# Second attention of a two-layer transformer: one product for the maxima of four heads, a start by groups, and gathers that wait for their tiles

## The chip, the core and the metric

The kernel runs on one core of one Trainium2 chip. The metric is the time of one execution on the device in microseconds (us); a median of several runs is given. The engines are TensorE (PE; its weight loads PEld), VectorE (DVE), ScalarE (ACT), GpSimd (POOL) and SyncE (SP, which here only issues DMAs). Each engine works through its own queue in order, and they wait for each other by semaphores.

## What is computed

x is 64 batches of 128 tokens of 128 channels, in float32. Two layers follow each other:

```
x = x + cross_attention(layernorm(x), keys/values from fside and ctx)      # 16 heads of 8, 248 keys
x = x + experts(layernorm(x))      # 8 experts, the two best of each token, SwiGLU
x = x + cross_attention(layernorm(x), keys/values from ctx)                # 16 heads of 8, 120 keys
x = x + experts(layernorm(x))      # 8 experts, the two best, GELU, rank 64
```

The attention of each is softmax(q k / sqrt(8)) v, with biases on q, k, v and the output.

## The kernel before

**Batches and groups.** `attention(layer, w, norm, first, aside)` (L228) is a generator that serves both layers; `first` tells the first from the second. A group is GB = 4 batches, and there are 16 groups (NG). One iteration `it` of its loop advances a software pipeline: maxima of batch `it`, shift of batch `it-1`, scores and exponentials of `it-2`, values of `it-3`, output steps of `it-3` to `it-5`. The order of instructions on PE, ACT, DVE and POOL is that of the code (a manual schedule); the two sets of work beside the attention (`Aside0`, `Aside1`) are called at fixed places of the iteration: routing, experts, norms, additions of gathered rows.

**Heads in row groups.** The 128 channels are four groups of 32 rows of the PE array (`ra`), with four heads each (`s`, NS = 4). A head's 8 channels lie among the 32 rows. The queries are kept four times, in `q4`, each masked by `hmask` to one head's channels (`prep_q`, L293). The keys are kept twice, in `K2` (`keys_of`, L207, on ACT), with `v = s // 2`; `K2` also has a row of ones through which the maxima are subtracted.

**Maxima and scores.** `max_bank` (L373) multiplies, for one row group, each of four masked queries with the keys of the batch: in the second attention 4 products of 120 columns into one PSUM bank, from which DVE takes four maxima per query (L385). `score_bank` (L401) does keys times shifted masked queries, two products of 256 columns; ACT takes the exponential (L409). `round_` pairs two row groups that do maxima with two that do scores; `rounds(0, 1)` of the second attention fills all eight PSUM banks. PSUM tiles come in turn from `mtile()`, eight banks.

**Shift.** `shift` (L430, L433) turns the maxima with two PE transposes, and DVE adds them into `q4`. The scores of that batch, in the next iteration's rounds, read it.

**Order in the second attention's iteration.** values and `out1` (L446, L455), `rounds(0, 1)`, one piece of the experts (L1385 to L1418), `prep(it, 0)`, `out3`, `out2` (L475, L462, L466, L468), `out4` (L482), a router call, `prep(it, 1)`, `shift`, `out5` (L487), norms and gathers. `prep` makes the next group ready: with j = it mod 4, keys at j = 1 (L202, L207), values and transposed inputs at j = 2 (L214, L221, L176, L177), queries at j = 3 (L289, L293).

**Start.** The second attention starts with `prep_batch(0)`, and makes its first four batches ready one by one in iterations 0 to 2 (L313 to L318); group 1 comes in iterations 1 to 3.

**Between the attentions.** `tile_stage` runs the first layer's experts over 71 tiles of 256 rows: SP fetches rows from `xs` (L1051), PE multiplies (L1085, L1098), and the results go to `ys` in DRAM (L1105). POOL had scattered the rows into `xs` by indirect DMAs (L783). Within it, `first_results` gathers the results of the first 8 batches from `ys` (L1127, POOL), adds them (L1139) and makes the norms of two groups. The gathers of the others (L1328) and their additions (L1340) run beside the second attention. The dependencies of scatters, fetches and first gathers are given by hand: a declaration that none is there in a group of instructions, and a helper `behind` that adds single ones. `lists_`, `rp`, `yb` are pools of buffers in SBUF.

Of the kernel before, what the change touches and what calls it, by code (L numbers as in the profile page):

```python
# [44 lines left out]
def transformer_kernel(ctx, tc, a, out):  # L45
# [34 lines left out]
    def attention_weights(p, names=("wq", "wk", "wv", "wo", "bq", "bk", "bv", "bo")):  # L80
        columns = {"bq": NS, "bk": NV}
        return {
            n: load_row(p + n, D) if n in ("bv", "bo")
            else load_const(p + n, [D, columns.get(n, D)], a[p + n])
            for n in names
        }
# [145 lines left out]
    def attention(layer, w, norm, first, aside):  # L232
# [5 lines left out]
        with ExitStack() as es:  # L238
# [9 lines left out]
            nm = NM  # L248

            src, q4s, xnTs, ps_, pavs, pts, ots, normed = {}, {}, {}, {}, {}, {}, {}, {}  # L250

# [23 lines left out]
            def mtile():  # L275
                return banks.tile([128, 512], F32, name="bank", tag="bank")

            def prep_x(g):
                xnT = work.tile([D, GB * S], F32, name="xnT", tag="xnT", bufs=1)
                norm.turned(normed.pop(g), mtile(), xnT)  # L280
                xnTs[g] = xnT
                q4s[g] = work.tile([128, GB, NS, S], F32, name="q4", tag="q4", bufs=3)

            pqs = {}

            def prep_q(g, v):
                if v == 0:
                    pqs[g] = mtile()
                    nc.tensor.matmul(pqs[g], lhsT=w["wq"], rhs=xnTs[g], start=True, stop=True)  # L289
                pq = pqs[g]  # L290
                for i in range(2):
                    s = 2 * v + i
                    nc.scalar.activation(  # L293
                        q4s[g][:, :, s, :], pq.rearrange("p (b q) -> p b q", b=GB),
                        AF.Identity, bias=w["bq"][:, s : s + 1], scale=hmask[:, s : s + 1],
                    )

            def prep_k(g):
                keys_of(w, src[g], g, n0, mtile())

            def prep_v(g):
# [21 lines left out]
            def prep(it, half):  # L323

                g, j = it // GB + 1, it % GB
                if not first:
                    if g == 1:
                        if (j, half) == (2, 1):
                            prep_v(1)
                        elif (j, half) == (1, 0):  # L330
                            prep_k(1)
                    elif g < NG:
                        pieces = (
                            (), (lambda: prep_k(g),),
                            (lambda: prep_v(g), lambda: prep_x(g)),
                            (lambda: prep_q(g, 0), lambda: prep_q(g, 1)),
                        )[j]
                        if half < len(pieces):
                            pieces[half]()
                    return  # L340
# [25 lines left out]
            def max_bank(b, ra, v):  # L366
# [5 lines left out]
                def mm(u, s):  # L372
# [8 lines left out]
                    for p in range(2)  # L381
                ]

                def reduce():
# [116 lines left out]
            if first:  # L501
                loads(0)
                yield
                context_k(0)
                yield
                context_v(0)
                loads(1)
                yield
                prep_k(0)
                prep_batch(0)  # L510
                yield
            else:
                prep_batch(0)
                loads(1)
            oTs, pos_ = {}, {}

            for it in range(B + 5):
# [13 lines left out]
                if first and it % GB == 2:  # L531
                    norm_of(it // GB + 2)
                if 2 <= it <= B + 1:
                    ps_[it - 2] = work.tile([128, nc_, 4, 512], F32, name="p", tag="p")
# [23 lines left out]
                else:  # L558
# [4 lines left out]
                    aside.piece(mtile)  # L563
                    if it < GB - 1:
                        prep_batch(it + 1)
                    prep(it, 0)
# [8 lines left out]
                    if it > GB and it % GB == 1:  # L575
                        norm_of(it // GB + 1)
                    if it == GB - 1:
                        normed[1] = READY[1]
                        prep_x(1)
                        prep_q(1, 0)  # L580
                        prep_q(1, 1)
                    aside.fetch_for(it)
# [184 lines left out]

    AFTER = mybir.DependencyInfo(mybir.DependencyClass.Sync, mybir.DependencyReason.DATA)
    DEEP = 4
    scatters, spare = [], []  # L770

    def behind(ins, earlier):
        for e in earlier:
            tc.add_manual_dep(ins.ins, e.ins.name, AFTER, reason="rows of one array")

    def scatter(probe, j, k, xn):
# [9 lines left out]
        if scatters:  # L786
            tc.declare_no_dep(s.ins, group="scatters", reason="rows of their own")
        behind(s, [scatters[-DEEP] if len(scatters) >= DEEP else spare[0]])
        tc.add_to_no_dep_group("scatters", s.ins)
# [50 lines left out]

    lists_ = ctx.enter_context(tc.tile_pool(name="lists", bufs=1))
    back = place.tile([S, B, 2], I32, name="back", tag="back")
# [179 lines left out]
    def tile_stage(work, mtile):  # L1022
# [14 lines left out]
        def fetch(t):  # L1037
# [9 lines left out]
            share = s[:, n + 3 * TT : n + 3 * TT + 2].rearrange("p (h d) -> p h d", h=2)  # L1047
            first_ = scatters[2 * GA * GB - DEEP : 2 * GA * GB]
            assert len(first_) == DEEP
            for dst, src in ((x, xs[bass.ds(r, TT), :D]), (share, xs[bass.ds(r, TT), bass.ds(e + D, 1)])):  # L1050
                f = nc.sync.dma_start(dst, src.rearrange("(h p) d -> p h d", p=S))  # L1051
                if t < NA:

                    tc.declare_no_dep(f.ins, group="scatters", reason="rows of the first groups")
                    behind(f, first_)
                    tc.add_to_no_dep_group("scatters", f.ins)
# [56 lines left out]
        def first_results(t):  # L1113
# [6 lines left out]
            if step == 0:  # L1120
# [4 lines left out]
                for b in range(2):  # L1125
                    for k in range(2):
# [3 lines left out]
                        )  # L1130
                        tc.declare_no_dep(g.ins, group="writes", reason="other tiles")
                        behind(g, needed)
                        groups.add("reads")
# [124 lines left out]

    rp = ctx.enter_context(tc.tile_pool(name="route", bufs=1))

# [26 lines left out]
    for g in range(4, NG):  # L1287
        load_x(g)
    l1 = attention_weights("a1_")
    wr1 = load_const("wgT", [D, E], a["wgT"])  # L1290
# [10 lines left out]
    with tc.manual_schedule(engines=ORDERED | {ET.SP}):  # L1301
        for _ in steps:
            pass


    class Aside1:


        def __init__(self, pool):
            self.pool, self.got, self.b, self.xn = pool, {}, 2 * GB, READY[0]  # L1310
            self.xnTs, self.gates, self.ready = {}, [], []
# [10 lines left out]
        def fetch(self, n):  # L1322
            for b in range(self.b, min(self.b + n, B)):
                if b % 2 == 0:
                    self.got[b // 2] = self.pool.tile([S, 2, 2, D], F32, name="yb", tag="yb", bufs=5)
                y = self.got[b // 2]
# [17 lines left out]

        def normed(self, j):

            return self.xn

        def made(self, b):
# [11 lines left out]
        def xnT_of(self, g):  # L1361
            self.xnTs[g] = self.pool.tile([D, GB * S], F32, name="xnT", tag="xnT", bufs=4)
            return self.xnTs[g]
# [81 lines left out]
def _laid_out(inp):  # L1445
# [29 lines left out]
    for p, l, names, tr in (  # L1475
# [6 lines left out]
        o[p + "wq"], o[p + "wk"] = moved(wq), moved(wk)  # L1482
        o[p + "bq"] = np.where(hm > 0, moved(bq).T, np.float32(0.0))
        o[p + "bk"] = np.where(km > 0, moved(bk).T, sm)
        o[p + "wv"], o[p + "bv"] = wv, bv
# [46 lines left out]
```

## Time and profile before

| What | us |
|---|---|
| Median of 3 runs (lowest, highest) | 1597.97 (1597.46, 1599.05) |
| The profiled execution | 1601.67 |
| Its span, first to last instruction | 1599.9 |
| Mean granted PE clock over the span | 0.959 |
| Second attention's share of the span, from its first transpose at 988.2 | 611.7 |
| L373, second attention: passes of 120 columns x2048 | 168.2 busy |
| L385, second attention: reductions x256 | 152.2 busy |
| L401, second attention: passes of 256 columns x2048 | 304.7 busy |

A row of the profile names line, engine, operation, what is written from what, shapes and count, then the busy time, the mean duration and the idle time of the engine ahead of it with what ended it. The time line gives start, duration and the merged count; in brackets stands the idle time before it. The slices show 40 equal parts of the span, and PEclk is the granted clock of PE in tenths. Busy times of matmuls overlap, since four row groups can work at once.

### The profile page before, as it was taken

How to read it: one execution, taken by the hardware profiler on the slowest of the kernel's cores; microseconds unless marked ns; L12 is line 12 of the kernel's file. 1: busy time of each engine (PE TensorE's matmuls, PEld its weight loads, DVE VectorE, ACT ScalarE, POOL GpSimd, SP SyncE). 2: the span in 40 equal slices, each digit the busy share in tenths (PEclk: the TensorE clock that was granted, in tenths of full speed). 3: DMA queues.
4: the chain of work that ended last, by engine and by line, in shares of the span. 5: the costliest groups of instructions: out<-in, count | busy, mean ns of one | idle time of the engine just before them, and what ended most of it. 6: DMA issues, size and time to landing. Idle time of an engine off the chain costs nothing.

```text
span 1599.9 us, 45004 instructions
## 1 busy us (share of the span) xinstructions
PE 1484.9 (93%) x18162; PEld 1182.0 (74%) x18162; DVE 1084.0 (68%) x2960; ACT 843.9 (53%) x1739; POOL 641.1 (40%) x1195
## 2 busy tenths in 40 slices
PE   7989999999999999888999998988999999999987
PEld 5767777777777777777888887767777777777765
DVE  6757888888888986454744443677666666667753
ACT  4646666666666655432333333666555555555643
POOL 4122255555565535443020302366554544443210
PEclk9999999999999999999999999799999989999999
DMA  8842122222222221466776664110111100000000
GB/s 218 228 115 59 48 57 56 62 60 60 60 60 59 53 71 44 133 190 186 202 212 193 201 186 127 30 32 21 37 31 29 31 29 28 27 27 15 15 8 27
DMA packets 143586, 133.22 MB, mean 83 GB/s; under 512 B 48402, under 2 KB 125970, under 8 KB 141458
## 3 DMA queue, kind: packets, MB, share of 16 engines
q1 hardware_dynamic: 135186, 113.02, 25.7%
q0 software_dynamic: 8192, 17.32, 3.5%
q8 instruction: 144, 2.36, 0.6%
q14 instruction: 64, 0.52, 0.1%
HBM read 97.31 MB, written 32.97 MB: 81 GB/s over the span
## 4 chain that ended last, share of the span: by engine, by line
PE 73%; DVE 10%; DMA 4%; issue 3%; SPq 3%; POOL 3%; ACT 3%; another core or an unknown queue 0%; POOLq 0%; ACTq 0%; DVEq 0%
PE bank L401 12%; PE bank L373 12%; PE bank L446 9%; PE bank L1085 9%; PE bank L1413 4%; PE bank L1392 4%; PE bank L1098 3%; DVE nm L385 3%; PE bank L289 2%; SPq L1247 2%; PE bank L1402 2%; PE bank L482 2%; DMA q<-xs 2%; PE bank L214 2%; PE bank L652 2%
## 5 line engine op out<-in xcount | busy, mean ns | idle before, releaser
L385 DVE TENSOR_REDUCE nm<-bank 128x2 f32<-128x496 f32 (+1 forms) x768 | 465.9, 664 | 141.3 <-PE bank L401 69.5
L401 PE MATMUL bank<-q,k 32*120 32x256 f32 (+1 forms) x3072 | 478.0, 408 | 16.4 <-DVE nm L385 5.0
L409 ACT ACTIVATE p<-bank 120x512 f32<-120x512 f32 (+1 forms) x768 | 403.3, 605 | 140.5 <-PE bank L401 106.0
L373 PE MATMUL bank<-k,q 32*128 32x248 f32 (+1 forms) x4096 | 462.4, 345 | 13.3 <-DMA k<-in_ctx_k 7.1
L373 PEld LDWEIGHTS bank<-k,q 32*128 32x128 f32 x4096 | 351.8, 191 | 81.6 <-issue 36.3
L401 PEld LDWEIGHTS bank<-q,k 32*120 32x120 f32 (+1 forms) x3072 | 302.0, 182 | 45.9 <-DVE nm L385 16.0
L446 PE MATMUL bank<-p,v 128*32 128x128 f32 (+1 forms) x4096 | 179.3, 279 | 4.6 <-DVE nm L385 3.9
L1090 DVE TENSOR_TENSOR p<-p,bank 128x256 f32<-128x256 f32 x213 | 87.8, 420 | 125.3 <-ACT p L1089 106.9
L155 POOL TENSOR_SCALAR rstd<-mv 128x4 f32<-128x4 f32 x32 | 6.3, 198 | 384.9 <-DVE mv L113 296.4
L783 POOL DMA_INDIRECT xs<-xn,at x128 | 129.4, 1011 | 28.5 <-issue 24.9
L455 ACT COPY ov<-bank 128x256 f32<-128x256 f32 x128 | 47.9, 375 | 170.5 <-PE bank L446 141.3
L1089 ACT ACTIVATE p<-bank 128x256 f32<-128x256 f32 x213 | 80.8, 385 | 102.4 <-PE bank L1085 92.4
L446 PEld LDWEIGHTS bank<-p,v 128*32 128x32 f32 (+1 forms) x4096 | 111.4, 111 | 29.6 <-issue 13.0
L1085 PE MATMUL bank<-q 128*128 128x256 f32 x516 | 122.4, 388 | 4.4 <-ACT oT L477 4.4
L433 DVE SCALAR_TENSOR_TENSOR q<-bank,c_smask,q 128x256 f32<-128x256 f32 x256 | 111.4, 477 | 12.7 <-PE bank L430 11.9
L1328 POOL DMA_INDIRECT yb<-ys,back x112 | 108.8, 971 | 27.7 <-issue 20.1
L167 POOL TENSOR_SCALAR xn<-x,mv,rstd 128x128 f32<-128x128 f32 x252 | 110.2, 447 | 7.5 <-issue 1.4
L293 ACT ACTIVATE q<-bank,c_a_bq,c_hmask 128x512 f32<-128x512 f32 x120 | 87.4, 787 | 45.3 <-PE bank L289 45.2
L1085 PEld LDWEIGHTS bank<-q 128*128 128x128 f32 x516 | 97.5, 196 | 17.0 <-ACT oT L477 4.8
L446 PE MATMUL bank<-p,vc 120*32 120x128 f32 x2048 | 104.2, 272 | 0.6 <-issue 0.5
L138 POOL TENSOR_TENSOR mv<-st 128x4 f32<-128x4 f32 x31 | 6.4, 206 | 205.4 <-DVE st L109 205.4
L1085 PE MATMUL bank<-vc 128*128 128x256 f32 x336 | 77.2, 379 | 0.0
(220 smaller groups left out, 2364.5 us busy)
## 6 DMA issues: line engine op xcount, KB each, us to landing
q<-in_w SPq DMA_DIRECT2D x43, 576.0 KB
vc<-in_w SPq DMA_DIRECT2D x28, 576.0 KB
vc<-in_ctx_v SPq DMA_DIRECT2D x16, 960.0 KB
ys<-zero SPq DMA_DIRECT2D x71, 128.0 KB
k<-in_ctx_k SPq DMA_DIRECT2D x32, 240.0 KB
q<-xs SPq DMA_DIRECT2D x43, 128.0 KB
ys<-q SPq DMA_DIRECT2D x43, 128.0 KB
x<-in_x SPq DMA_DIRECT2D x16, 256.0 KB
```

Of the source, the lines that this page charges most:

```text
L167: nc.gpsimd.tensor_scalar(xn[:, j, :D], xg[g][:, j, :], self.mv[:, b, 0:1], self.rstd[:, b : b + 1], ALU.add, ALU.mult,)
L293: nc.scalar.activation(q4s[g][:, :, s, :], pq.rearrange("p (b q) -> p b q", b=GB), AF.Identity, bias=w["bq"][:, s : s + 1], scale=hmask[:, ...
L373: nc.tensor.matmul(pa[:, u, :], lhsT=q4s[g][r, j, s, :], rhs=k2[g % 2][r, s // 2, j, :], start=True, stop=True,)
L385: nc.vector.tensor_reduce(nm[b % 2].rearrange("q i (a s) -> q a i s", s=16)[:, 2 * ra + v : 2 * ra + v + len(slots) // 2, :, 0], pa.rearra ...
L401: nc.tensor.matmul(pb[:n, v * 256 : (v + 1) * 256], lhsT=k2[g % 2][r, v, j, k0 : k0 + n], rhs=q4s[g][r, j, 2 * v : 2 * v + 2, :].rearrange ...
L409: nc.scalar.activation(ps_[b][:n, c, ra, :], pb[:n], AF.Exp, scale=SCALE)
L433: nc.vector.scalar_tensor_tensor(q, pm, smask[:, v : v + 1], q, ALU.mult, ALU.add)
L446: nc.tensor.matmul(pav[32 * ra : 32 * ra + 32, v * S : (v + 1) * S], lhsT=vs[g % 2][c][:, j, 4 * v + ra, i, :], rhs=p[:n, c, ra, (2 * v + ...
L783: s = nc.gpsimd.indirect_dma_start(xs, bass.IndirectOffsetOnAxis(at[:, j, k : k + 1], 0), xn, None)
L1085: nc.tensor.matmul(ph[:, u, :], lhsT=w[:, c, u * 128 : (u + 1) * 128], rhs=xT, start=True, stop=True)
L1090: nc.vector.tensor_tensor(hT[:, c, :], sa, ph[:, 1, :], ALU.mult)
L1328: nc.gpsimd.indirect_dma_start(y[:, k, b % 2, :], None, ys, bass.IndirectOffsetOnAxis(back[:, b, k : k + 1], 0),)
```

## The change

The second attention gets an unmasked copy of the queries, `qf` (one more ACT operation per group, bias `bqf`), and per group a copy of the keys for each of the four heads, `k4`, made by four DVE multiplications with `hmask`. The maxima of a row group are then one product of 480 columns. Groups 0 and 1 are made ready as whole groups: group 0 ahead of the loop, group 1 in iterations 0 and 1. The dependencies of scatters, fetches of tiles and first gathers are kept with `keep=`, in place of `behind`. A pool for lists is closed before the second attention; three sets of buffers get one buffer fewer (`q4` in the second attention, `yb`, `xnT` beside it).

```diff
+                if not first:
+                    qfs[g] = work.tile([128, GB, S], F32, name="qf", tag="qf")
...
+                if v == 0 and not first:
+                    nc.scalar.activation(
+                        qfs[g], pq.rearrange("p (b q) -> p b q", b=GB), AF.Identity,
+                        bias=w["bqf"],
+                    )
...
+            def prep_heads(g):
+
+                k4s[g] = work.tile([128, NS, GB, KC], F32, name="k4", tag="k4")
+                for s in range(NS):
+                    nc.vector.tensor_scalar(
+                        k4s[g][:, s], k2[g % 2][:, s // 2], hmask[:, s : s + 1], None, ALU.mult
+                    )
...
                     if g == 1:
-                        if (j, half) == (2, 1):
+                        if (j, half) == (0, 0):
+                            prep_k(1)
                             prep_v(1)
-                        elif (j, half) == (1, 0):
-                            prep_k(1)
+                        elif (j, half) == (0, 1):
+                            prep_x(1)
+                        elif j == 1:
+                            prep_q(1, half)
+                            if half:
+                                prep_heads(1)
                     elif g < NG:
                         pieces = (
-                            (), (lambda: prep_k(g),),
+                            (), (lambda: prep_k(g), lambda: prep_heads(g)),
                             (lambda: prep_v(g), lambda: prep_x(g)),
                             (lambda: prep_q(g, 0), lambda: prep_q(g, 1)),
                         )[j]
...
+                if not first:
+
+                    parts = [
+                        lambda: nc.tensor.matmul(
+                            pa, lhsT=qfs[g][r, j, :], rhs=k4s[g][r, :, j, :], start=True, stop=True
+                        ),
+                        lambda: None,
+                    ]
...
-                prep_batch(0)
+
+                ps_[0] = work.tile([128, nc_, 4, 512], F32, name="p", tag="p")
                 loads(1)
+                for g in range(2):
+                    normed[g] = READY[g]
+                prep_x(0)
+                prep_heads(0)
+                prep_q(0, 0)
+                prep_q(0, 1)
...
-                    if it < GB - 1:
-                        prep_batch(it + 1)
...
-                    if it == GB - 1:
-                        normed[1] = READY[1]
-                        prep_x(1)
-                        prep_q(1, 0)
-                        prep_q(1, 1)
...
-            tc.declare_no_dep(s.ins, group="scatters", reason="rows of their own")
-        behind(s, [scatters[-DEEP] if len(scatters) >= DEEP else spare[0]])
+            tc.declare_no_dep(
+                s.ins, group="scatters", keep=[scatters[-DEEP].ins] if len(scatters) >= DEEP else [],
+                reason="rows of their own",
+            )
...
-                    tc.declare_no_dep(f.ins, group="scatters", reason="rows of the first groups")
-                    behind(f, first_)
+                    tc.declare_no_dep(
+                        f.ins, group="scatters", keep=[s.ins for s in first_],
+                        reason="rows of the first groups",
+                    )
...
-                        tc.declare_no_dep(g.ins, group="writes", reason="other tiles")
-                        behind(g, needed)
+                        tc.declare_no_dep(
+                            g.ins, group="writes", keep=[w.ins for w in needed], reason="other tiles"
+                        )
```

`first_`, the scatters that a fetch of tiles waits for, was the last four of the first ten groups and is now all 80.

More of the change, by code (lines that the diff above doesn't have):

```diff
@@ L80, in attention_weights @@
     def attention_weights(p, names=("wq", "wk", "wv", "wo", "bq", "bk", "bv", "bo")):
-        columns = {"bq": NS, "bk": NV}
+        columns = {"bq": NS, "bk": NV, "bqf": 1}
         return {
@@ L248, in attention @@
             nm = NM
+            qfs, k4s = {}, {}
             src, q4s, xnTs, ps_, pavs, pts, ots, normed = {}, {}, {}, {}, {}, {}, {}, {}
@@ L281, in prep_x @@
                 xnTs[g] = xnT
-                q4s[g] = work.tile([128, GB, NS, S], F32, name="q4", tag="q4", bufs=3)
+                q4s[g] = work.tile([128, GB, NS, S], F32, name="q4", tag="q4", bufs=3 if first else 2)
+                if not first:
+                    qfs[g] = work.tile([128, GB, S], F32, name="qf", tag="qf")
             pqs = {}
@@ L532, in attention @@
                     norm_of(it // GB + 2)
-                if 2 <= it <= B + 1:
+                if 2 <= it <= B + 1 and it - 2 not in ps_:
                     ps_[it - 2] = work.tile([128, nc_, 4, 512], F32, name="p", tag="p")
@@ L766, in transformer_kernel @@
     filled = []
-    AFTER = mybir.DependencyInfo(mybir.DependencyClass.Sync, mybir.DependencyReason.DATA)
     DEEP = 4
     scatters, spare = [], []
-    def behind(ins, earlier):
-        for e in earlier:
-            tc.add_manual_dep(ins.ins, e.ins.name, AFTER, reason="rows of one array")
     def scatter(probe, j, k, xn):
@@ L837, in dispatch @@
             rt.last.append(lambda probe, j=j: [scatter(probe, q0 + j, k, made[j // GB][:, j % GB, :]) for k in range(2)])
-    lists_ = ctx.enter_context(tc.tile_pool(name="lists", bufs=1))
+    rp = ctx.enter_context(tc.tile_pool(name="route", bufs=1))
+    until_tiles = ctx.enter_context(ExitStack())
+    lists_ = until_tiles.enter_context(tc.tile_pool(name="lists", bufs=1))
     back = place.tile([S, B, 2], I32, name="back", tag="back")
@@ L1047, in fetch @@
             share = s[:, n + 3 * TT : n + 3 * TT + 2].rearrange("p (h d) -> p h d", h=2)
-            first_ = scatters[2 * GA * GB - DEEP : 2 * GA * GB]
-            assert len(first_) == DEEP
+            first_ = scatters[: 2 * GA * GB]
+            assert len(first_) == 2 * GA * GB
             for dst, src in ((x, xs[bass.ds(r, TT), :D]), (share, xs[bass.ds(r, TT), bass.ds(e + D, 1)])):
@@ L1257, in rest @@
                 pass
-    rp = ctx.enter_context(tc.tile_pool(name="route", bufs=1))
     wr0 = const.tile([D, 3 * E], F32, name="c_wqkvT", tag="c_wqkvT")
@@ L1288, in transformer_kernel @@
         load_x(g)
-    l1 = attention_weights("a1_")
+    l1 = attention_weights("a1_", ("wq", "wk", "wv", "wo", "bq", "bqf", "bk", "bv", "bo"))
     wr1 = load_const("wgT", [D, E], a["wgT"])
@@ L1303, in transformer_kernel @@
             pass
+    until_tiles.close()
     class Aside1:
         def __init__(self, pool):
-            self.pool, self.got, self.b, self.xn = pool, {}, 2 * GB, READY[0]
+            self.pool, self.got, self.b = pool, {}, 2 * GB
             self.xnTs, self.gates, self.ready = {}, [], []
@@ L1324, in fetch @@
                 if b % 2 == 0:
-                    self.got[b // 2] = self.pool.tile([S, 2, 2, D], F32, name="yb", tag="yb", bufs=5)
+                    self.got[b // 2] = self.pool.tile([S, 2, 2, D], F32, name="yb", tag="yb", bufs=4)
                 y = self.got[b // 2]
@@ L1343, in lead @@
                 norms[2].roots(b + 1 - GB, b + 1)
-        def normed(self, j):
-            return self.xn
         def made(self, b):
@@ L1361, in xnT_of @@
         def xnT_of(self, g):
-            self.xnTs[g] = self.pool.tile([D, GB * S], F32, name="xnT", tag="xnT", bufs=4)
+            self.xnTs[g] = self.pool.tile([D, GB * S], F32, name="xnT", tag="xnT", bufs=3)
             return self.xnTs[g]
@@ L1483, in _laid_out @@
         o[p + "bq"] = np.where(hm > 0, moved(bq).T, np.float32(0.0))
+        if tr:
+            o[p + "bqf"] = moved(bq).T
         o[p + "bk"] = np.where(km > 0, moved(bk).T, sm)
```

## The prediction

> **What bounds the kernel now.** I read the page first, then the stretches of the second attention, then its order of time engine by engine.
>
> ```profile
> PE 1484.9 (93%) x18162; PEld 1182.0 (74%) x18162; DVE 1084.0 (68%) x2960; ACT 843.9 (53%) x1739; POOL 641.1 (40%) x1195
> ...
> PEclk9999999999999999999999999799999989999999
> ...
> L373 PE MATMUL bank<-k,q 32*128 32x248 f32 (+1 forms) x4096 | 462.4, 345 | 13.3 <-DMA k<-in_ctx_k 7.1
> ```
>
> TensorE is the bound, but "93% busy" counts overlapping, waiting passes. A float32 product shows as two passes: 16 products per batch and layer make the 4096 of L373. The table by stretch (PE, PEld, DVE, ACT, POOL busy; granted clock; DMA) shows what the page averages away:
>
> ```profile
> 988.00:1017.00 29.00, 22.38 (x180) 17.82 (x182) 10.90 (x23) 12.12 (x28) 13.12 (x16) 0.59 0.19 56
> ...
> 1302.00:1310.00 8.00, 7.95 (x105) 6.22 (x104) 3.42 (x13) 3.62 (x8) 6.68 (x8) 1.00 0.18 55
> 1310.00:1313.40 3.40, 2.54 (x13) 1.46 (x11) 1.58 (x3) 2.30 (x3) 3.01 (x4) 1.00 0.19 58
> 1313.40:1320.20 6.80, 6.57 (x56) 4.80 (x60) 5.08 (x12) 3.61 (x8) 2.08 (x3) 0.50 0.08 22
> ```
>
> The start of the second attention runs at a clock of 0.59. Once per group of four batches PE trickles (13 passes in 3.4 us), and then runs at half clock for 6.8 us. The half-clock stretches after 1129 us add up to 72 us, so at most 36 us of loss. The rest of this stage is a chain through PE, ACT and DVE that decides what added work costs. Here is iteration j=1 of a group, DVE and then PE:
>
> ```profile
> 1294.55 0.42 DVE L1418 TENSOR_TENSOR x<-x,bank 128x256 f32<-128x256 f32 x1 [0.81 <-PE bank L1413]
> 1295.68 0.26 DVE L466 RECIPROCAL rs<-bank 128x16 f32<-128x16 f32 x1 [0.71 <-PE bank L462]
> 1295.97 0.29 DVE L468 TENSOR_TENSOR o<-bank,rs 128x128 f32<-128x128 f32 x1
> 1296.19 0.88 DVE L433 SCALAR_TENSOR_TENSOR q<-bank,c_smask,q 128x256 f32<-128x256 f32 x2
> ```
>
> ```profile
> 1295.70 0.38 PE L430 MATMUL bank<-ident,nm 128*128 128x128 f32 x2
> 1295.92 0.60 PE L176 MATMUL bank<-ident,xn 128*128 128x128 f32 x4
> 1296.45 1.08 PE L446 MATMUL bank<-p,v 120*32 120x128 f32 x32
> 1297.46 0.36 PE L373 MATMUL bank<-k,q 32*128 32x120 f32 x1
> ```
>
> L433 (the shift by the maxima) ends at 1297.07, and the next rounds start at 1297.46. Their score products read what L433 wrote, so L433 has only 0.4 us of slack, and whatever stands ahead of it in DVE's queue goes to PE beyond that.
>
> **The change, part by part.**
>
> **1. Maxima in one product.** Before, one row group of 32 gets 4 products of 120 columns per batch, 8 passes. Three passes of two row groups in turn take 0.38 us against 0.27 for one, so they start 0.055 us apart and a row group takes one every 0.11: 8 x 0.11 = 0.90 us. After, it gets 2 passes of 480 columns. The nearest row is L1392, eight passes of 512 columns in 3.60 us:
>
> ```profile
> 1299.88 3.60 PE L1392 MATMUL bank<-xnT,c_lw1T 128*128 128x512 f32 x8
> 1297.67 0.38 PE L373 MATMUL bank<-k,q 32*128 32x120 f32 x3
> ```
>
> (3.60 - 0.61)/7 = 0.427 us each, so 0.40 for 480 columns and 0.80 for two. Weight loads were mostly hidden already; a visible one costs 0.09 (0.36 against 0.27), and one of two goes. So 0.1 to 0.2 us per batch, not a factor of four: the columns stay, the other rows work on scores at 4 x 0.21 us meanwhile. I take 0.15 in the 36 iterations whose rounds don't start on a wait named below: -5 us (all 64 at 0.2: -13; none: 0). DVE's four reductions (L385, 0.65 each) and ACT's four exponentials stay.
>
> **2. Keys of each head (prep_heads): 4 added DVE operations of 128x480 per group.** No such row exists. Nearest, SBUF to SBUF with a per-partition scalar:
>
> ```profile
> L931 DVE TENSOR_SCALAR used<-used,row_number x1: 439/439/439, 733.9 to 733.9; 128x264 f32<-128x264 f32 x1
> ...
> L125 DVE TENSOR_SCALAR xn<-x,mv,rstd x4: 330/972/1792, 5.1 to 9.6; 128x128 f32<-128x128 f32 x4
> ```
>
> From 128 elements (330 ns, the undisturbed one) to 264 (439) is 0.8 ns an element; L931 carried on at one element per 0.96 GHz cycle gives 439 + 216/0.96 = 664 ns. Against this stands the Trainium skill, "VectorE: DVE Perf Modes", section "Mode 2×_2P — use both read ports for one tensor": such a float32 operation, one tensor source and all in SBUF, moves two elements a cycle. That would be 250 ns of streaming and about 160 of fixed cost: 0.41 us. The row is nearer to this operation, so I take 0.66, i.e. 2.65 us per group.
> Place: in the queue it stands after L468 and ahead of L433, in j=1. K2 is there in time (its two ACT writes, L207, end at 1296.07 and 1296.75). So L433 would end at 1296.26 + 2.65 + 0.88 = 1299.8 instead of 1297.07, and the scores start near 1299.9: 2.4 us late. Behind L433 wait L487, L112 and L113; POOL's L155 waits for L113, but has idled 150 us there already. PE is in order, so the first maximum may run, and then the next score product's weight load blocks everything. 14 groups x 2.4 = +34 us. By the skill's rate 1.45 us each, +20; with POOL in the way (L125's median 972 ns) 3.7 each, +52.
>
> **3. The unmasked query: one added ACT operation of 128x512 per group,** like L293 (two in 1.45 us): 0.73 us. It goes ahead of the four L293. Order of time at j=3 to j=0 (ACT, then the weight load):
>
> ```profile
> 1071.14 1.47 ACT L293 ACTIVATE q<-bank,c_a_bq,c_hmask 128x512 f32<-128x512 f32 x2
> ...
> 1072.44 0.17 PEld L401 LDWEIGHTS bank<-q,k 32*120 32x120 f32 x1 [0.52 <-ACT q L293]
> ```
>
> Here PE already waits for the last L293. The new maxima don't need the masked queries, but the bank that those five read is the eighth before the rounds' second maximum, of eight banks; so the rounds still wait for the last. +0.73 x 14 = +10 us (0 if the bank isn't what holds them).
>
> **4. Trickle.** 64 maximum passes and weight loads a batch become 16, so fewer instructions stand in the trickle (rounds of 3.9 to 4.8 us where others take 2.3). What starves PE there is not named by the profile ("issue"). I take -0.7 us x 12 groups = -8 (0 to -20).
>
> **5. Start by groups.** From the last tile (988.2 us) to the rounds of batch 4 (1022.7) pass 34.5 us, among them four waits of PE on ACT's copies (1.4 to 2.4 us) and at 1016.6 the first full clock. Four chains of transpose, copy, product and four 128-wide queries become one of 512 width; against that stand five ACT operations of 0.75 ahead of the first maxima, group 1's keys, values and queries in iterations 0 and 1, and 2.65 us of heads ahead of the first shift. Iterations at the old half clock would then stand near 993, 999.5, 1007, 1014 and 1018: -5 us (-10 to +3).
>
> **6. Gathers, scatters, fetches.** POOL issues the first gathers at 817.8 and 826.4 us, though the tiles they name are written at 851.8 and 887.6: before, they do not wait. After, they do; behind them on POOL stand only their own additions and norms, and on DVE their statistics. For the second, 887.6 + 2.2 (landing) + 5.1 (four gathers of 1.27) + 3.6 = 898.5 against statistics due at 900.7: hidden by 2 us, as is the fourth. Scatters that wait for the fourth one before: issues 1.3 us apart give 5.2 us for a landing of 2 to 4. SP's fetches wait for scatters that ended long ago. 0, at most +4. Smaller buffers (yb, xnT, q4): each is freed an iteration before its next use, 0.
>
> **7. Clock.** "TensorE: Matmul & The Clock Gate" of the Trainium skill, section "HAM oscillation — how this bites in real kernels", asks for an idle gap beyond about 3.4 us before the clock falls; a new 2.4 us stall would then cost nothing. The row 1310.00:1313.40 has PE busy 2.54 of 3.40 us and the clock still falls, so the trace asks for less. Emptier stretches: up to 14 x 1.7 = +24; trickle gone: -36. I take 0.
>
> Sum: -5 + 34 + 10 - 8 - 5 = +26 us. The profiled execution took 1601.7 (span 1599.9), so 1627.7; its median sibling 1598.0, so 1624.
>
> **Rivals.**
> - *The trickle goes, and the clock stays up* (faster). Place: the j=3 rounds and the L1402 behind them. All of it is worth 12 x 1.7 (rounds) + 18 (the waits within L1402, 1.5 each) + 36 (clock) = 74 us; with two thirds gone, -49, against the +34 of the other terms without the trickle: about 1583. It decides once more than about half goes. For it: fewer passes in that place. Against: POOL's gathers stand there too and stay.
> - *DVE at two elements a cycle and a hidden query:* +20 - 5 - 8 - 5 = +2, 1600, about no change.
> - *The long passes hold each other up:* if PE kept passes of different row groups strictly in order, a round would gain about 0.7 us, 64 x 1.4 = +90, 1690. The trace speaks against it: score passes start 0.01 us behind a maximum's first pass, while its second follows 0.2 later.
> - *The clock falls in the new stalls too:* 1624 + 20 = 1645.
>
> **Numbers.** Chances: the sum as taken 0.50; clock stays up 0.27; about no change 0.09; strict order 0.03; clock falls oftener 0.11. A measurement of this kernel tells about 0.2% from no change. Faster 0.30, same 0.05, slower 0.65. The range reaches from the faster rival to beyond the fourth: 1582 to 1650; the likeliest case alone is 1605 to 1645.
>
> **What would show it.** The four new DVE operations near 0.66 us (or 0.41) right ahead of L433 in j=1, and rounds waiting for DVE there; PE waiting for ACT's last query in j=0, 0.7 us longer; rounds of 2.2 us elsewhere; half-clock stretches as many as before; L1127 after 853 us; rounds of batch 4 near 1018. I'd be wrong if the half-clock stretches vanish, or the shift has slack that I overlooked.

## The result, and the profile after

| | before | after |
|---|---|---|
| Median (lowest to highest), us | 1597.96 (1597.46 to 1599.05), 4 runs | 1582.92 (1580.04 to 1587.09), 4 runs |
| Profiled execution, its span, us | 1601.67, 1599.9 | 1582.29, 1580.5 |
| Mean granted PE clock | 0.959 | 0.973 |

The ratio is 0.9892, with a 95% interval of 0.9863 to 0.9921: the change made the kernel 1.1% faster on this chip (1582.9 us, against a forecast of 1624). On two other chips the same two kernels stand the other way round (below), so "faster" is only half of the result.

The page after, its engines, the granted clock, and the row that stands for the second attention's part of L373:

```profile
PE 1442.8 (91%) x16620; PEld 1118.6 (71%) x16620; DVE 1106.3 (70%) x3024; ACT 849.7 (54%) x1740; POOL 641.3 (41%) x1195
...
PEclk9989999999999999899999999899999999999999
...
L407 PE MATMUL bank<-k,qf 32*128 32x480 f32 x512 | 150.8, 604 | 1.3 <-ACT qf L295 0.8
```

2048 passes of 120 columns (168.2 us busy) became 512 of 480 (150.8): the columns stay, as predicted. In the table by stretch, the start and the rest of the second attention:

```profile
993.70:1020.30 26.60, 20.64 (x158) 11.26 (x158) 16.76 (x38) 15.16 (x24) 13.47 (x16) 0.81 0.20 59
...
1050.00:1580.50 530.50, 472.72 (x5127) 347.25 (x5127) 378.30 (x1135) 304.40 (x583) 231.99 (x355) 0.96 0.09 26
```

From the last tile to the rounds of batch 4 pass 26.6 us at a clock of 0.81 (34.6 us at 0.65 before). The forecast had the rounds of batch 4 near 1018; they start at 1020.3, though the last tile is 5.5 us later than before.

**The unit for everything that follows is the iteration.** Iteration `it` runs from its first value product (L446 before, L475 after) to the next one's; j = it mod 4. Iterations 17 to 58 repeat group by group. The table has the mean length in us (10.5 groups), with the stages around them; the rows of j are means of single iterations:

| | before | after | before, second kind | after, second kind |
|---|---|---|---|---|
| the last tile's last PE pass starts at | 987.2 | 992.7 | 967.9 | 972.7 |
| from there to iteration 8 | 56.4 | 47.9 | 55.1 | 47.2 |
| iterations 8 to 16 | 60.7 | 61.0 | 54.9 | 59.1 |
| iterations 17 to 58 | 389.8 | 375.8 | 341.4 | 352.4 |
| of these j = 0 | 6.40 | 7.26 | 6.90 | 7.22 |
| j = 1 | 7.77 | 7.63 | 7.80 | 7.63 |
| j = 2 | 10.00 | 11.31 | 10.00 | 11.31 |
| j = 3 | 13.03 | 9.50 | 7.67 | 7.19 |
| iteration 59 to the end | 105.8 | 103.1 | 105.7 | 104.0 |
| span | 1599.9 | 1580.5 | 1525.1 | 1535.4 |

"Second kind" is another chip (e9 and e12 below). The kernel before was timed in six sets of runs: in three it took 1598, 1609 and 1608 us (called the first kind of chip here), in three 1523, 1524 and 1524 us (the second kind). The length of j = 2 agrees to 0.01 us between the kinds; within iterations 17 to 58 the difference lies in j = 3, with some of it given back in j = 0.

### The profile page after: what moved, and what is told of

It is laid out like the page before. It is cut to its first block, busy times and chain, and to the rows that moved or that the text cites. A ratio compares the mean times of both kernels' runs of the same rounds, so it can differ in the third digit from the quotient of the medians.

```text
span 1580.5 us, 41996 instructions
## 1 busy us (share of the span) xinstructions
PE 1442.8 (91%) x16620; PEld 1118.6 (71%) x16620; DVE 1106.3 (70%) x3024; ACT 849.7 (54%) x1740; POOL 641.3 (41%) x1195
## 4 chain that ended last, share of the span: by engine, by line
PE 66%; DVE 15%; DMA 6%; SPq 5%; issue 3%; ACT 3%; POOL 3%; another core or an unknown queue 0%; POOLq 0%; ACTq 0%; DVEq 0%
PE bank L430 10%; PE bank L475 9%; PE bank L1115 8%; PE bank L394 8%; PE bank L1420 4%; PE bank L1441 4%; DVE nm L414 3%; PE bank L1128 3%; DMA q<-xs 3%; SPq L1278 2%; PE bank L407 2%; PE bank L292 2%; DVE q L462 2%; PE bank L511 2%; PE bank L681 2%
## 5 line engine op out<-in xcount | busy, mean ns | idle before, releaser
L430 PE MATMUL bank<-q,k 32*120 32x256 f32 (+1 forms) x3072 | 444.5, 401 | 14.8 <-DVE nm L414 5.0
L430 PEld LDWEIGHTS bank<-q,k 32*120 32x120 f32 (+1 forms) x3072 | 298.3, 182 | 61.9 <-DVE nm L414 16.6
L394 PE MATMUL bank<-k,q 32*128 32x248 f32 x2048 | 294.3, 403 | 12.5 <-DMA k<-in_ctx_k 11.8
L394 PEld LDWEIGHTS bank<-k,q 32*128 32x128 f32 x2048 | 203.1, 190 | 59.7 <-issue 23.0
L475 PE MATMUL bank<-p,v 128*32 128x128 f32 (+1 forms) x4096 | 179.6, 279 | 1.8 <-DVE h L1435 0.6
L407 PE MATMUL bank<-k,qf 32*128 32x480 f32 x512 | 150.8, 604 | 1.3 <-ACT qf L295 0.8
L475 PEld LDWEIGHTS bank<-p,v 128*32 128x32 f32 (+1 forms) x4096 | 111.2, 110 | 26.1 <-issue 13.2
L462 DVE SCALAR_TENSOR_TENSOR q<-bank,c_smask,q 128x256 f32<-128x256 f32 x256 | 111.1, 475 | 10.3 <-PE bank L459 9.6
L475 PE MATMUL bank<-p,vc 120*32 120x128 f32 x2048 | 104.2, 272 | 0.6 <-issue 0.5
L1157 POOL DMA_INDIRECT kvT<-ys,back x16 | 15.4, 962 | 197.5 <-DMA vc<-xs 118.1
```

The source lines that it names most:

```text
L394: nc.tensor.matmul(pa[:, u, :], lhsT=q4s[g][r, j, s, :], rhs=k2[g % 2][r, s // 2, j, :], start=True, stop=True,)
L407: lambda: nc.tensor.matmul(pa, lhsT=qfs[g][r, j, :], rhs=k4s[g][r, :, j, :], start=True, stop=True),
L430: nc.tensor.matmul(pb[:n, v * 256 : (v + 1) * 256], lhsT=k2[g % 2][r, v, j, k0 : k0 + n], rhs=q4s[g][r, j, 2 * v : 2 * v + 2, :].rearrange ...
L462: nc.vector.scalar_tensor_tensor(q, pm, smask[:, v : v + 1], q, ALU.mult, ALU.add)
L475: nc.tensor.matmul(pav[32 * ra : 32 * ra + 32, v * S : (v + 1) * S], lhsT=vs[g % 2][c][:, j, 4 * v + ra, i, :], rhs=p[:n, c, ra, (2 * v + ...
```

## The experiments

A round is the work of `round_`: the maxima of two row groups beside the scores of two others. Theory P came first: the one product pays by shorter rounds (2.32 to 1.95 us) and fewer stretches at half clock. Rival S: the start and the dependencies are the gain. Theory G came after e5: a stall of some chips, in j = 3 where the gathers run, costs the kernel before more than the changed one. Ratios are to the kernel before on the same chip, with a 95% interval.

### What each part is worth (first kind of chip)

**e1_old_maxima**: without the one product.

```diff
-                    parts = [ lambda: nc.tensor.matmul(pa, lhsT=qfs[g][r, j, :], rhs=k4s[g][r, :, j, :], ...), lambda: None ]
...
-                    nc.scalar.activation(qfs[g], ...)
...
-                (lambda: prep_k(g), lambda: prep_heads(g)),
+                (lambda: prep_k(g),),
```

> The changed kernel with the maxima of before (sixteen products of 32x120 from masked queries; no qf, no k4, no head operations); its start by groups and its dependencies stay. Theory P (the one product pays: a round goes from 2.32 to 1.95 us since the weight loads of the score products are hidden once the maxima's are a quarter; fewer stretches at half clock): rounds back to 2.3 us, half-clock stretches back to about 12 pieces or 70 us, time 1595 to 1605 us. Rival S (the start and the order of the dependencies are the gain, the maxima pay only for their own preparation): 1578 to 1587, rounds of any length. The prediction's own terms (-5 maxima, +34 heads, +10 query) say it is 39 us faster than the changed kernel: 1544.

1604.4 us, ratio 0.9964 (0.9951 to 0.9977). Iterations 17 to 58 take 393.6 us with j = 3 at 13.23, as before the change. Most of the gain is the maxima's; rival S falls. The start, the dependencies and the smaller buffers are in this kernel too, so none of them is what shortens j = 3.

**e2_old_start**: `prep_batch` and group 1 as before, all else changed.

> The changed kernel with the start of before (batch by batch: four chains of transpose, copy, product and queries; group 1 prepared where it was), maxima and dependencies as changed. Theory P: only the start's 8 us are lost, about 1591 us, rounds stay 1.95 us and half-clock stretches after 1050 us stay near 37 us. Rival S: back to 1597 or more.

1591.2, ratio 0.9898 (0.9880 to 0.9916). The time to iteration 8 is 55.3 us against 47.9, so the start's 7.4 us show in the trace; the ratio, not apart from the changed kernel's, neither confirms nor excludes them.

**e3_deps_only**: the kernel before with `keep=[...]` in place of `behind(...)`.

> The kernel before with nothing but the changed dependencies of scatters, fetches and gathers. Theory P: the first attention and the tiles get 0 to 5 us longer (the changed kernel's last tile is written 5.5 us later), nothing after them changes: 1598 to 1603. Rival S: below 1590. If the 5.5 us are a matter of one execution and not of the dependencies: 1598, with the last tile at 988 us.

1610.3, ratio 1.0001 (0.9982 to 1.0020): no effect on the time that can be told, though its last tile starts its last pass at 993.7, as late as in the changed kernel.

**e4_heads_late**: the four head operations behind the shift.

```diff
                     on(1, shift)
                     on(5, out5)
+                    if it % GB == 1 and it // GB + 1 < NG:
+                        prep_heads(it // GB + 1)
                     aside.ahead(it)
```

> The changed kernel with the four head operations behind the shift and the residual of the same iteration on DVE instead of ahead of them. Theory P (they cost 0.75 us a group there, since the scores of the next rounds wait for the shift): 14 x 0.75 = 10 us faster, 1573. By the prediction's 2.4 us a group: 1549. If DVE then keeps the reductions of the next rounds and so the banks from PE instead: 1580 to 1590, with longer waits of PE for reductions in j=2.

1595.4, ratio 0.9928 (0.9901 to 0.9956), no faster. The wait of the score products' weight loads for L462 fell from 11.4 to 4.9 us (1050 to 1560), and those of the experts' transpose of the gates (L1413 of the changed kernel) for DVE and ACT rose from 8.8 to 16.2: j = 2 stays at 11.32. DVE is late either way.

### Doubling the suspects (second kind of chip)

**e5_after_again**: the changed kernel unaltered.

> The changed kernel once more, unaltered, so that it is known in more rounds and on the chip of the three variants beside it: ratio to the kernel before 0.986 to 0.992. Its last expert tile is to end near 993 us if the 5.5 us later end of the first half is a trait of the kernel, near 988 if it was one execution's.

1536.8 against 1523.3, ratio 1.0083 (1.0062 to 1.0104): slower. That refuted P as a whole: the rounds were 1.95 us here too.

**e6_heads_spread**: `prep_heads(g, ((), (0,), (1, 2), (3,))[it % GB])` behind `out5`.

> The changed kernel with the four head operations of a group spread: none in j=0, one in j=1, two in j=2, one in j=3, each behind the shift and the residual on DVE. Theory P1 (the heads cost where they hold up the shift, and the late version only moved the 3 us burst of DVE onto the next rounds' reductions and the experts' banks): small pieces find room, 0.75 x 14 = 10 us faster than the changed kernel, ratio about 0.983. Theory P2 (DVE's whole work between two uses of a bank is the limit there, so each microsecond on DVE costs wherever it stands): same as the changed kernel within 3 us.

1548.8, ratio 1.0157 (1.0130 to 1.0183): slower than the changed kernel, which neither theory had. j = 2 fell to 10.58, but j = 0 rose to 8.72: its first maximum needs the last head, which stands behind the shift and statistics. The time line of an iteration with j = 0:

```profile
1210.93 0.44 DVE L314 TENSOR_SCALAR k<-k,c_hmask 128x480 f32<-128x480 f32 x1
...
1211.49 0.18 PEld L406 LDWEIGHTS bank<-k,qf 32*128 32x128 f32 x1 [2.43 <-ACT ov L483]
```

The bracket names ACT's copy, which ends at 1211.38; the head ends at 1211.37. In other iterations the maxima don't wait for that copy.

**e7_heads_twice**: `for s in 2 * list(range(NS))` in the same place.

> The changed kernel with the four head operations done twice in the same place (eight of 0.46 us). Theory P (0.75 us a group on the path of 1.85 us of work, the shift having about 1.1 us of slack): the second four have no slack, +1.85 x 14 = +26 us, 1609 against 1583. If the operations fill gaps of DVE: under +8 us. By the prediction's 0.66 us each: +37.

1561.7, ratio 1.0246 (1.0220 to 1.0271). j = 2 is 13.19 in the mean, so four more operations of 0.466 us (1.86) cost 1.88. That looks like no slack at all, as theory P had it, but the mean hides two cases. Two j = 2 iterations (18 and 34), 11.5 us long in the changed kernel:

```profile
1092.66:1105.69 13.03, 10.87 (x93) 7.11 (x92) 9.31 (x30) 7.44 (x17) 7.21 (x12) 1.00 0.08 21
1233.05:1246.79 13.74, 12.39 (x94) 7.80 (x93) 9.35 (x30) 7.71 (x17) 7.89 (x12) 0.88 0.12 33
```

In five of the eleven the clock stays up, and the four operations cost 1.52 us; in six it falls to a half for 3.4 us, and they cost 1.96 to 2.49. So 0.34 us of the 1.86 find room, and the rest of the 1.88 is the clock. PE's and its weight loads' waits in the second of the two:

```profile
PE bank L430 <- DVE q L462: 1.3, 1, 1.3
...
PEld bank L430 <- DVE q L462: 2.1, 1, 2.1
```

**e8_query_twice**: the qf operation made twice.

> The changed kernel with the unmasked query made twice (two ACT operations of 0.69 us ahead of the four masked ones, same result). The prediction held that each costs its 0.73 us on PE's wait for the last query, +10 us for 14 groups. Theory P (hidden: the waits for qf come to 2.4 us in all, those for the masked queries to 1.7): 0 to +4 us.

1541.6, ratio 1.0111 (1.0087 to 1.0135). j = 0 rose from 7.22 to 7.60: 0.38 us of an operation of 0.69. That lies between the prediction (all of it) and theory P (hidden); the two intervals of e5 and e8 overlap, so it rests on the traces.

### The stall in j = 3

**e9_before_again** and **e12_after_third**: both kernels unaltered, beside each other.

> The kernel before, unaltered, for its trace on the chip of the three beside it. The changed kernel was 0.989 of it in the first comparison and 1.008 on a chip on which both are faster (1537 and 1523 us). Theory G (a stall that exists on some chips only, in the j=3 iterations where the gathers run, costs the kernel before about 5 us for each of 12 groups and the changed one about half): time near 1523 us goes with j=3 iterations of 7 to 8 us and at most three half-clock stretches after 1050 us; time near 1600 with iterations of 11 to 14.5 us and some 12 stretches. Rival R (the chips differ evenly over the whole kernel): all stages scale by the same 4 to 5%.

> The changed kernel, unaltered, beside the others on their chip. Theory G: ratio to the kernel before 0.985 to 0.99 where that takes about 1600 us, 1.005 to 1.01 where it takes about 1523.

1526.1, ratio 1.0017 (1.0001 to 1.0034), which also shows how well a kernel repeats itself; 1535.9, ratio 1.0072 (1.0052 to 1.0091). Theory G's numbers hold within iterations 17 to 58, and rival R falls: there j = 1 and j = 2 agree to 0.03 us. Up to the last tile the kinds differ by another 20 us, which no run here explains.

How the stall looks: one pair of iterations (j = 2, j = 3) of the kernel before on the first kind, and on the second. Columns: stretch, its length, busy PE, PEld, DVE, ACT, POOL with counts, granted clock, DMA share, GB/s.

```profile
1259.97:1270.07 10.10, 9.96 (x118) 7.39 (x117) 6.31 (x22) 7.38 (x17) 7.28 (x12) 1.00 0.17 45
1270.07:1282.94 12.87, 11.08 (x123) 7.92 (x122) 7.10 (x17) 5.42 (x9) 7.86 (x9) 0.73 0.13 38
```

```profile
1214.34:1224.43 10.09, 9.96 (x118) 7.40 (x117) 6.30 (x22) 7.35 (x17) 7.27 (x12) 1.00 0.16 45
1224.43:1232.09 7.66, 7.31 (x122) 5.72 (x121) 6.11 (x15) 4.85 (x8) 6.34 (x8) 1.00 0.16 47
```

j = 2 is the same; j = 3 does the same PE work in 5.2 us more, part of it at half clock. Within such a j = 3 on the first kind, in order of time:

```profile
1123.64 0.95 POOL L1328 DMA_INDIRECT yb<-ys,back  x1 [0.30 <-issue]
...
1124.49 0.37 ACT L455 COPY ov<-bank 128x256 f32<-128x256 f32 x1 [2.45 <-PE bank L401]
...
1126.62 0.37 PE L401 MATMUL bank<-q,k 32*120 32x256 f32 x1 [0.74 <-issue]
...
1127.11 1.53 POOL L1340 TENSOR_TENSOR x<-x,yb 128x256 f32<-128x256 f32 x2
...
1128.08 0.26 PE L373 MATMUL bank<-k,q 32*128 32x120 f32 x1 [0.84 <-issue]
...
1128.12 2.35 DVE L385 TENSOR_REDUCE nm<-bank 128x4 f32<-128x480 f32 x4 [4.43 <-PE bank L401]
```

and the same instructions on the second kind:

```profile
1096.55 0.37 ACT L455 COPY ov<-bank 128x256 f32<-128x256 f32 x1 [0.73 <-PE bank L446]
...
1097.41 0.95 POOL L1328 DMA_INDIRECT yb<-ys,back  x1 [0.30 <-issue]
...
1097.54 2.35 DVE L385 TENSOR_REDUCE nm<-bank 128x4 f32<-128x480 f32 x4
...
1098.40 0.90 PE L1402 MATMUL bank<-gT,c_select 32*128 32x128 f32 x4
```

The gathers are issued at the same places. On the first kind, PE falls behind the second from 2.3 to 3.0 us into the iteration on (in all ten, 19 to 55), about when the first gather's rows arrive (2.5 to 2.6 us). It issues in bursts, here 0.74 and 0.84 us apart, with nothing that it waits for ("issue"), and ACT's copy of finished values comes 2.9 us after the iteration's start (1.6 to 2.9 in the ten) instead of 1.2.

**e10_before_no_gathers** and **e11_after_no_gathers**: without the gathers and their additions (in the kernel before L1328 and L1340).

```diff
-                    nc.gpsimd.indirect_dma_start(y[:, k, b % 2, :], None, ys, ...)
...
-                    nc.gpsimd.tensor_tensor(x, x, y[:, k], ALU.add)
```

> The kernel before without the 112 gathers of the second attention and without the additions that use them (batches 8 to 63 are computed without the experts' output of the first layer). Theory G (the gathers' transfers or their issue starve PE in the same iterations): on a chip where the kernel before takes about 1600 us, 50 to 70 us less, the j=3 iterations 7 to 8 us and few half-clock stretches; on a chip where it takes 1523, 0 to 10 us less. Rival R (the dense short products themselves or the chip, not the gathers): 0 to 10 us less on either chip, j=3 iterations as long as before.

> The changed kernel without the 112 gathers of the second attention and without the additions that use them (same part left out). Theory G: on a slow chip 20 to 35 us less, so that it ends slower than the kernel before without gathers by about 0.8%; on a fast chip 0 to 10 us less. Rival R: 0 to 10 us less on either.

On the second kind: 1519.0, ratio 0.9972 (0.9955 to 0.9990), and 1526.9, ratio 1.0017 (1.0000 to 1.0033). Little to gain there, as G says, and the changed kernel stays the slower one, by 7.9 us.

**e14_before_no_gathers** and **e15_after_no_gathers** repeated them on another chip, of the second kind again.

> The same as the earlier run of the kernel before without the second attention's gathers and their additions, in the hope of the other kind of chip. If the kernel before takes about 1600 us here: theory G, about 1520 (the j=3 iterations at 7.7 us as on the fast chips); rival R, 1590. If it takes about 1523: 1519 again, and nothing new.

> The same for the changed kernel: where the kernel before takes about 1600 us, theory G says about 1530, 0.5 to 0.8% slower than the kernel before without gathers; rival R 1575. Where it takes about 1523: 1527 again.

1518.7, ratio 0.9961 (0.9938 to 0.9983); 1527.3, ratio 1.0024 (1.0009 to 1.0039). On the second kind the gathers still cost something in iterations 8 to 16, in both pairs: the kernel before takes 54.9 us there with them and 50.0 without, the changed one 59.1 and 51.0.

**e18_before_no_gathers** came to a chip of the first kind.

> The kernel before without the second attention's gathers and their additions, a third time, still for a chip on which the kernel before takes about 1600 us. There theory G says about 1520, rival R 1590; on the other kind of chip 1519 again.

1542.4 against 1607.9, ratio 0.9596 (0.9578 to 0.9613): 65 us. The same pair of iterations:

```profile
1226.19:1236.28 10.09, 9.95 (x117) 7.39 (x116) 6.31 (x22) 7.36 (x17) 4.43 (x8) 1.00 0.14 38
1236.28:1243.95 7.67, 7.32 (x122) 5.72 (x121) 6.11 (x15) 4.86 (x8) 0.00 (x0) 1.00 0.02 5
```

j = 3 takes 7.67 us, with no half clock: to 0.01 us what the second kind takes with its gathers. Without the gathers and their additions the stall is gone (rival R falls); the kind of chip decides whether they cause it. It is unlikely that the additions start it: in nine of the ten iterations they end by 0.8 us into j = 3 or start at 5.5 and later (3.6 in the tenth; 1127.11 in the rows above, after the first gap of PE), and PE falls behind in between. No run leaves out the additions alone. What differs in the chip, and by what path the gathers reach PE, stays open.

### Can the heads' cost be had back?

**e13_heads_on_pool** (second kind): `nc.gpsimd.tensor_scalar`, two at the end of j = 1 and two at the end of j = 2.

> The changed kernel with the four head operations of a group on POOL instead of DVE, two at the end of j=1 and two at the end of j=2. Iterations with j=2 are 1.1 to 1.45 us longer in the changed kernel than in the kernel before, on every chip. Theory H (that is the heads on DVE, whose shift and bank releases come later): j=2 iterations back to 9.9 to 10.1 us, 14 x 1.2 = 17 us faster than the changed kernel: ratio to the kernel before 0.997 where the changed kernel is 1.008, 0.978 where it is 0.989. Rival B (the shorter rounds reach the experts' products before DVE has released the banks, whoever makes the heads): j=2 stays at 11 to 11.5 us, ratio as the changed kernel's. If POOL slows DVE's operations while it works: slower than the changed kernel.

1552.3, ratio 1.0173 (1.0146 to 1.0200). j = 2 is 10.33 instead of 11.31, so the heads on DVE are most of what lengthens it (theory H), but j = 3 rose from 7.19 to 9.78, and the kernel is slower than the changed one. DVE in a j = 3:

```profile
1208.54 0.29 DVE L112 BATCH_NORM_STATS2 st<-x 128x6 f32<-128x128 f32 x1 [1.96 <-POOL x L1373]
...
1209.08 0.65 DVE L413 TENSOR_REDUCE nm<-bank 128x4 f32<-128x480 f32 x1
```

One head takes POOL 1.49 us; its additions (L1373) come later, DVE's statistics wait for them, and the reductions queued behind those start later.

**e16_heads_split** and **e17_heads_on_act** (first kind): two at the end of j = 1 and two at the end of j = 2, on DVE, and on ACT (`nc.scalar.activation(k4, k2, AF.Copy, scale=hmask)`).

> The changed kernel with two head operations on DVE at the end of j=1 and two at the end of j=2, behind shift and residual. Seen so far: all four late in j=1 give back nothing (j=2 at 11.0 and 11.55 us); one in j=1, two in j=2 and one in j=3 bring j=2 to 9.95 and 10.97 but cost 2.5 us in j=0, whose first maximum waits for the last; on POOL they bring j=2 to 9.95 and 10.59, but DVE's statistics then wait 2 us in j=3 for POOL's additions. Theory D (DVE has room for two at a time, and only the order costs): j=2 at 10.0 to 11.0, j=3 7.5, j=0 as in the changed kernel: 5 to 8 us faster than it. Rival: the same microseconds turn up in j=3, no gain.

> The same places, but on ACT (a scaled copy of the keys in SBUF, same result), which is idle at the start of an iteration until the first values are done. Theory D': j=2 near 9.95 and 10.6, j=3 and j=0 as in the changed kernel, 14 us faster than it: ratio to the kernel before 0.998 where the changed kernel is 1.008, 0.98 where it is 0.989, so that it beats both on both kinds of chip. Rival: ACT's copies and exponentials come later by the 1.4 us and PE waits for them: as slow as the changed kernel or slower.

1584.0, ratio 0.9844 (0.9815 to 0.9873), and 1594.8, ratio 0.9914 (0.9897 to 0.9932). j = 2 falls to 10.69 and 10.39, but j = 3 rises to 10.53 and 12.70 (changed kernel: 9.50): that the microseconds turn up in j = 3 is what the rival of e16 said, and theory D' fails. In e17 the heads end 1.65 us into j = 3 (19, 23 and 27), ACT's copy of the values, which stood at 1.2 to 1.5 in the changed kernel, follows at 2.9 to 4.6, and the score products wait for it:

```profile
PE bank L431 <- ACT ov L485: 14.7, 8, 3.5
```

(PE's waits from 1050 to 1560.) This kernel has the changed kernel's rounds with their few passes, and still its j = 3 is nearly as long as before the change (13.03). e16 is the lowest ratio measured on the first kind, but its interval overlaps the changed kernel's and it didn't run beside it; nor was either tried on the second kind. A version that beats both kernels on both kinds is not shown.

## Why the prediction was wrong

The sum failed in two places. The stall (terms 4 and 7) gave it the wrong sign on the first kind of chip; the heads were over-costed and the maxima under-credited on both. The table compares profiled spans, in us; the split of terms 1 to 3 is for 14 groups:

| Step | predicted | measured |
|---|---|---|
| 1 maxima | -5 | -13, as what remains |
| 2 heads | +34 | +21 |
| 3 unmasked query | +10 | +5 |
| 1 to 3 together, iterations 8 to 58 | +39 | +15 (second kind); +12 without the gathers |
| 4 and 7, trickle and clock | -8 and 0 | -29 together on the first kind, 0 on the second |
| 5 start | -5 | -8 on both |
| 6 gathers and the rest up to the last tile | 0 | +5.5 and +4.8 |

The parts give 15 - 8 + 5 = +12 on the second kind, where the spans differ by +10.3 (1.7 us are won back after iteration 59); on the first kind, with the same 15 for terms 1 to 3, 2.7 us won back after iteration 59 and -29, they give the -19 of the spans. Of the +15 some 3 us belong to the gathers in iterations 8 to 16, since without them (e10 and e11) the two kernels differ by 11.8; so the terms 1 to 3 themselves come to +12.

- **Term 4 is the step that failed.** "I take -0.7 us x 12 groups" was a guess at something that the profile called "issue", with a range of 0 to -20. The comparison of kinds gives its size: iterations 8 to 58 of the kernel before take 54 us more on the first kind (5.8 + 48.4), those of the changed one 25 (1.9 + 23.4). So 29 us went, clock included. The rival "the trickle goes, and the clock stays up" named the place and the direction. That its 1583 was met is luck: it took 49 us of gain and 34 of other costs, where 29 and about 10 were measured, and its reason ("fewer passes in that place") is not enough, since e17 has as few.
- **Why the changed kernel stalls less** is in part open. e1 shows that it comes with the one product and its preparation. In the trace of the changed kernel PE falls behind only from 3.6 us into j = 3 on, in the experts' select products (L1430; six groups), or not before 7.0 (four groups): its rounds are over by then. That this is the reason is argued, not isolated.
- **Term 7** went with it. After iteration 8 the half-clock stretches fell from 72 to 38 us, on the second kind they are 14 and 17. They follow the stalls. The row weighed against the Trainium skill ("TensorE: Matmul & The Clock Gate", "HAM oscillation — how this bites in real kernels") was the better guide: on the second kind the doubled heads, which leave PE idle for 1.2 to 1.3 us in each j = 2, already raised them from 17 to 34 us.
- **Term 2.** A head took 0.464 us, so the row L931 (0.66) was the wrong one and the skill's two elements per cycle ("VectorE: DVE Perf Modes", "Mode 2×_2P — use both read ports for one tensor"; estimate 0.41) the nearer. (One element per 0.96 GHz cycle, with which L931 was carried on, fits other rows of DVE in the kernel before: L1090 takes 420 ns for 256 columns and L1407 683 for 512, 1.03 ns an element.) The place was right: four more cost 1.52 us where the clock stays up, 14 x 1.52 = 21, if the first four cost as much as the second four. The prediction's own rule (2.4 us late for 2.65 of work) gives 1.6 for the 1.86 measured, so of this term only the duration was mis-sized.

The heads in the time line of the changed kernel (e12), with what waits for them:

```profile
1218.90 1.60 DVE L313 TENSOR_SCALAR k<-k,c_hmask 128x480 f32<-128x480 f32 x4
...
1220.42 0.87 DVE L462 SCALAR_TENSOR_TENSOR q<-bank,c_smask,q 128x256 f32<-128x256 f32 x2
...
1220.95 0.17 PEld L430 LDWEIGHTS bank<-q,k 32*120 32x120 f32 x1 [0.55 <-DVE q L462]
```

They stand ahead of the shift, as forecast, and the score products wait for the shift's first half.

- **Term 3.** The queries are the path at j = 0, but only 0.38 of 0.69 us.
- **Term 1.** Per group j = 0 to 3 changed by +0.32, -0.17, +1.31 and -0.48, together +0.98. Less 1.52 and 0.38 the maxima come to -0.92, 0.23 an iteration instead of 0.15 in 36 of them. In a round of 1.95 us the score passes of a row group start 0.21 us apart after the first; before, they alternated 0.31 and 0.22. So "weight loads were mostly hidden already" did not hold for every second score pass of a row group.
- **Term 6.** That the first gathers did not wait before, and now do, came true:

```profile
817.82 1.00 POOL L1127 DMA_INDIRECT kvT<-ys,back  x1 [80.92 <-DVE p L1090]
```

```profile
858.88 1.00 POOL L1157 DMA_INDIRECT kvT<-ys,back  x1 [118.11 <-DMA vc<-xs]
```

The first row is of the kernel before, the second of the changed one. But kernels with the changed dependencies come later to their last tile: 992.7 to 995.8 against 987.2 and 988.4 on the first kind, 969.5 to 974.1 against 967.9 and 968.3 on the second. In the changed kernel 4 us of it are a wait for the keys of group 1 (iteration 4 of the first attention), which SP issues behind 71 fills of `ys`: at 92.3 us in e12, at 87.8 in e9. The trace of e3, with the dependencies alone, has that wait too: PE waits 11.9 us for these keys, against 7.1 in the kernel before. So it comes with the dependencies; why SP is later is not shown, and e3's median doesn't show the loss.

Without the stall the prediction's direction holds: on both chips of the second kind on which the changed kernel ran it is slower (1.0083 and 1.0072), by half of the forecast 1.6%.

## What to carry to other kernels

Cut a pipelined kernel's trace into its iterations by their place in the period: lengths that repeat to 0.01 us show at once which iteration a change or a chip touches. Don't give a small number to a wait that the profile calls "issue": bound it by an iteration that does the same work without it, which was there to see (iteration 59, after the last gather, took 7.67 us where the others took 11.5 to 14.5). When a rival's time is met, look whether its terms were met too. A move of work to an idle engine is priced by what that engine's queue delays, and a gain of 1% can turn with the chip.

## What the hardware showed that was not expected

- The same program takes 1598 to 1609 us on some chips and 1523 to 1524 on others. In the second attention it comes with indirect gathers of 128 rows: while they arrive PE issues in bursts with nothing that it waits for, and ACT and DVE start late too. 65 us hang on 112 gathers and their additions there, 5 us on the other kind.
- DVE multiplies 128x480 float32 in SBUF by a per-partition scalar in 0.464 us; POOL takes 1.49.
- PE's clock fell to a half for 3.4 us after PE had been busy for 2.1 to 2.2 of the 3.4 us before, with one gap of 1.2 to 1.3 us (e7, in eight of its groups; in the others the same gap left the clock up).
